# Spacing the rows of every output store 31 x 128 KiB apart instead of 31 x 4 KiB in a pairwise bilinear kernel

## The chip, the cores and the metric

The kernel runs on one core of one Trainium2 chip. The metric is the device time in microseconds (us). TensorE multiplies matrices, VectorE (DVE in profiles) works element by element, DMA engines move data; HBM is the memory off the cores, SBUF and PSUM are a core's own. Medians are quoted with the number of runs; runs are marked fast or slow, and only fast runs are compared.

## The reference

```python
# r_inputs: (4096, 32, 64) float32; W: (496, 64, 64) float32; 496 = pairs i < j of 32 fields
i_idx, j_idx = np.triu_indices(32, k=1)
vi = inputs[:, i_idx, :]
vj = inputs[:, j_idx, :]
vdotw = jnp.einsum('bpd,pde->bpe', vi, W)
y = (vdotw * vj).reshape(B, -1)          # (4096, 31744) float32
```

The output has 4096 rows of 31744 x 4 = 126,976 bytes, together 520.09 MB. The inputs that the kernel reads are 33.55 MB of x and 8.39 MB of weights. It is a kernel that mostly writes.

## The kernel before

A tile is 128 batch rows, one per partition; there are 32 tiles. Per tile TensorE transposes x and multiplies it with the weights into PSUM, DVE multiplies with the second field and writes the result into a ring in SBUF, and five stores (`STORES` groups the columns) take it from there. The parts that matter:

```python
STORES = [[0, 1], [2, 3], [4, 5], [6, 7, 8], [9, 10, 11, 12, 13, 14, 15]]
RING = 28160                    # float32 elements per partition, about 4.4 stores
# ... cut ...
    def load_x(t):
        xt = xbuf[t % 2]
        nc.scalar.dma_start(out=xt[:, : F * D], in_=x[ts(t, P), :])
        return xt
# ... cut: weights are loaded once, the first tile is transposed ...
    for t in range(NT):
        # ... cut: load of the next tile's x ...
        for s, group in enumerate(STORES):
            if at + store_w[s] > RING:
                at = 0
            osb = ring[:, at : at + store_w[s]]
            at += store_w[s]
            o0 = off[2 * group[0]]
            # ... cut: matmuls into PSUM, DVE products from PSUM and x into osb ...
            nc.sync.dma_start(out=out[ts(t, P), o0 : o0 + store_w[s]], in_=osb)
```

`out` is (4096, 31744), so partition p of tile t writes into batch row 128 t + p, and neighbouring partitions of a store write 124 KiB apart. This distance is called the pitch below.

## Time and profile before

| | before |
|---|---|
| median, 6 runs | 1339.76 us (1339.70 to 1339.98) |
| profiled span | 1338.1 us |
| DMA traffic | 562.89 MB, 421 GB/s over the span |
| share of the 16 DMA engines' time in packets | 92.7% stores and weights, 6.0% x loads |
| DVE busy | 1199.8 us, 90% |
| median landing of the largest store, 3776 KB | 21.9 us |

The lines are quoted and worked through in the prediction below.

### The profile page before, as it was taken

The page shows a single profiled execution, that of the slowest core. Times are in us where ns is not written, and L with a number is a line of the kernel's source. Part 1 is how long each engine was busy: PE and PEld are TensorE (multiplying, and loading weights), DVE is VectorE, ACT ScalarE, POOL GpSimd, SP SyncE. Part 2 cuts the span into 40 slices and gives each one's busy share as a digit, 9 for nine tenths or more (in the row PEclk, how much of TensorE's full clock was granted, in tenths as well). Part 3 has the DMA queues.
Part 4 walks back from the last instruction along what each step waited for, and adds up shares of the span by engine and source line. Part 5 has one row for each costly group of instructions (what it writes and reads, how often), then busy time and mean ns, then how long its engine had stood idle before and what let it go on. Part 6 is the DMA issues. An engine that isn't in the chain of part 4 may idle for free.

```text
span 1338.1 us, 13157 instructions
## 1 busy us (share of the span) xinstructions
PE 1142.4 (85%) x5376; PEld 511.0 (38%) x5376; DVE 1199.8 (90%) x1376; ACT 66.1 (5%) x65; POOL 0.9 (0%) x8
## 2 busy tenths in 40 slices
PE   7899788898988988988889888889788898988982
PEld 3344333343344433433333334434344333433431
DVE  6999899898899988999889989899898998998993
ACT  1000000000000000000000000000000000000000
POOL 0000000000000000000000000000000000000000
PEclk9999999999998999999999999999999999999996
DMA  9999999999999999999999999999999999999996
GB/s 393 427 430 433 431 427 435 424 428 432 430 430 428 424 425 430 421 429 430 416 427 415 428 433 403 429 422 423 430 418 411 431 417 432 411 424 432 422 424 272
DMA packets 30012, 562.89 MB, mean 421 GB/s; under 512 B 3456, under 2 KB 3840, under 8 KB 5376
## 3 DMA queue, kind: packets, MB, share of 16 engines
q1 hardware_dynamic: 25344, 528.49, 92.7%
q10 hardware_dynamic: 4608, 33.56, 6.0%
q8 instruction: 42, 0.69, 0.2%
q14 instruction: 18, 0.15, 0.0%
HBM read 41.94 MB, written 520.09 MB: 420 GB/s over the span
## 4 chain that ended last, share of the span: by engine, by line
DMA 41%; DVE 39%; PE 16%; issue 2%; DVEq 0%
DMA out_dram<-ring 41%; DVE ring L155 35%; PE pring L145 13%; DVE ring L164 4%; PE pring L102 3%; DMA x<-in_x_dram 1%; DVEq L155 0%; DVEq L164 0%
## 5 line engine op out<-in xcount | busy, mean ns | idle before, releaser
L155 DVE TENSOR_TENSOR ring<-pring,x 128x1024 f32<-128x1024 f32 (+3 forms) x1056 | 1115.8, 1102 | 115.3 <-DMA out_dram<-ring 55.9
L145 PE MATMUL pring<-w,xT 64*128 64x512 f32 (+4 forms) x4864 | 1077.5, 560 | 165.7 <-DVE ring L155 161.4
L145 PEld LDWEIGHTS pring<-w,xT 64*128 64x128 f32 x4864 | 452.5, 189 | 758.6 <-DVE ring L155 601.3
L103 ACT COPY xT<-pring 128x1024 f32<-128x1024 f32 x64 | 64.8, 1013 | 1193.8 <-PE pring L102 1193.8
L164 DVE TENSOR_TENSOR ring<-pring,x 128x64 f32<-128x64 f32 (+3 forms) x320 | 114.5, 383 | 3.7 <-DVE ring L155 0.5
L102 PE MATMUL pring<-ident,x 128*128 128x128 f32 x512 | 73.6, 290 | 8.5 <-DMA x<-in_x_dram 8.5
L102 PEld LDWEIGHTS pring<-ident,x 128*128 128x128 f32 x512 | 58.5, 147 | 46.9 <-issue 36.9
L103 ACT ACT_TABLE_LOAD x1 | 1.3, 1283 | 1.7 <-PEq L198 1.7
masks.py:199 POOL TENSOR_SCALAR_AFFINE_SELECT ident<-ident 128x128 f32<-128x128 f32 x1 | 0.3, 294 | 0.0
L78 POOL MEMSET x<- 128x64 f32 x2 | 0.2, 152 | 0.0
masks.py:197 POOL MEMSET ident<- 128x128 f32 x1 | 0.2, 205 | 0.3 <-POOLq L198 0.3
L198 POOL MEMSET const-bfloat16-1.0<- 128x1 bf16 x1 | 0.1, 102 | 0.0
L198 POOL MEMSET const-uint8-127<- 128x1 uint8 x1 | 0.1, 102 | 0.0
L198 POOL MEMSET const-float32-0.0<- 128x1 f32 x1 | 0.1, 99 | 0.2 <-issue 0.2
L198 POOL MEMSET const-float32-1.0<- 128x1 f32 x1 | 0.1, 99 | 0.0
## 6 DMA issues: line engine op xcount, KB each, us to landing
out_dram<-ring SPq DMA_DIRECT2D x32, 3776.0 KB, 21.9
out_dram<-ring SPq DMA_DIRECT2D x32, 3264.0 KB, 21.6
out_dram<-ring SPq DMA_DIRECT2D x32, 3168.0 KB, 22.4
out_dram<-ring SPq DMA_DIRECT2D x32, 2912.0 KB, 21.4
out_dram<-ring SPq DMA_DIRECT2D x32, 2752.0 KB, 22.0
x<-in_x_dram ACTq DMA_DIRECT2D x32, 1024.0 KB, 14.2
w<-in_w_dram SPq DMA_DIRECT2D x1, 992.0 KB, 7.5
w<-in_w_dram SPq DMA_DIRECT2D x1, 928.0 KB, 11.8
```

Source lines behind the costliest of these rows:

```text
L78: nc.gpsimd.memset(xb[:, F * D :], 0.0)
L102: nc.tensor.transpose(pt[:, ts(c, P)], xt[:, ts(n * g + c, P)], ident)
L103: nc.scalar.copy(xT[:, ts(g, 2 * BANK)], pt)
L145: nc.tensor.matmul(pm[:, h * half + b0 : h * half + b1], xT[h * D : (h + 1) * D, ts(p, P)], w_sb[p][h * D : (h + 1) * D, c0 + b0 : c0 + b1 ...
L155: nc.vector.tensor_tensor(runs(osb, o[0], o[1], n[0]), runs(pm, 0, half, n[0]), runs(xt, xj[0], xj[1], n[0]), ALU.mult,)
L164: nc.vector.tensor_tensor(osb[:, o[h] : o[h] + n[h]], pm[:, h * half : h * half + n[h]], xt[:, xj[h] : xj[h] + n[h]], ALU.mult,)
L198: nc = bacc.Bacc("TRN2", target_bir_lowering=False, num_devices=1)
```

## The change

Each partition takes 32 neighbouring batch rows, one per tile: partition p of tile t now owns batch row 32 p + t. The host reorders x so that each tile's load is still one contiguous 1 MB block, and the output is declared as (128, 32 x 31744), which is the same memory under another shape. The intent is to alter one thing only, the distance between the 128 rows of a store.

```diff
-    B = x.shape[0]
-    NT = B // P
+    NT = x.shape[0]
 ...
+    cols = sum(width)
 ...
-        nc.scalar.dma_start(out=xt[:, : F * D], in_=x[ts(t, P), :])
+        nc.scalar.dma_start(out=xt[:, : F * D], in_=x[t])
 ...
-            nc.sync.dma_start(out=out[ts(t, P), o0 : o0 + store_w[s]], in_=osb)
+            nc.sync.dma_start(out=out[:, t * cols + o0 : t * cols + o0 + store_w[s]], in_=osb)
 ...
-    x = np.ascontiguousarray(r_inputs).reshape(B, F * D)
+    NT = B // P
+    x = np.ascontiguousarray(r_inputs.reshape(P, NT, F * D).transpose(1, 0, 2))
 ...
-    o_d = nc.dram_tensor("out_0_dram", (B, NP * D), F32, kind="ExternalOutput").ap()
+    o_d = nc.dram_tensor("out_0_dram", (P, NT * NP * D), F32, kind="ExternalOutput").ap()
 ...
-    return r.results[0]["out_0_dram"]
+    return r.results[0]["out_0_dram"].reshape(B, NP * D)
```

## The prediction

> **What bounds the kernel now.** I read the page's head and its slices first, to see which resource never rests.
>
> ```profile
> span 1338.1 us, 13157 instructions
> PE 1142.4 (85%) x5376; PEld 511.0 (38%) x5376; DVE 1199.8 (90%) x1376; ACT 66.1 (5%) x65; POOL 0.9 (0%) x8
> ...
> DVE  6999899898899988999889989899898998998993
> ...
> DMA  9999999999999999999999999999999999999996
> GB/s 393 427 430 433 431 427 435 424 428 432 430 430 428 424 425 430 421 429 430 416 427 415 428 433 403 429 422 423 430 418 411 431 417 432 411 424 432 422 424 272
> DMA packets 30012, 562.89 MB, mean 421 GB/s; under 512 B 3456, under 2 KB 3840, under 8 KB 5376
> ```
>
> The DMA row stands at 9 in every slice but the last, and the GB/s row is flat near 427. DVE is busy too, but 10% of its time is free. So the candidate is DMA, and the table of queues says what fills it.
>
> ```profile
> q1 hardware_dynamic: 25344, 528.49, 92.7%
> q10 hardware_dynamic: 4608, 33.56, 6.0%
> q8 instruction: 42, 0.69, 0.2%
> ...
> HBM read 41.94 MB, written 520.09 MB: 420 GB/s over the span
> ```
>
> The shares add to 98.9% of 16 engines' span: 1323 us of 1338.1 are packets. Queue 1 is the stores and the weights, queue 10 the x loads. Queue 1's packets are 32 x 5 x 128 = 20480 store rows, 16 x 128 = 2048 weight rows, and 16 completions for each of 176 transfers, 2816: together 25344. So each row of a store is one packet, 520.09 MB / 20480 = 25.4 KB on average. Its speed: 528.49 MB / 16 = 33.03 MB per engine in 0.927 x 1338.1 = 1240 us is 26.6 GB/s per engine, 426 GB/s for sixteen. The x loads give 33.56 / 16 / (0.060 x 1338.1) = 26.1 GB/s, nearly the same, though they read rather than write. That both directions run at one speed speaks for the engines as the limit and against HBM.
>
> The waits agree that compute stands behind the stores.
>
> ```profile
> DVE ring L155 <- DMA out_dram<-ring: 55.9, 35, 3.0
> DVE ring L155 <- PE pring L145: 30.7, 27, 12.9
> ...
> PE pring L102 <- DMA x<-in_x_dram: 8.5, 1, 8.5
> ```
>
> DVE waits 35 times for a store to give back a piece of the ring; the only long wait for x is the first load. Last I asked for stretches, to find the 1.1% in which DMA rests (columns: PE, PEld, DVE, ACT, POOL busy, granted clock, DMA share, GB/s).
>
> ```profile
> 0.00:8.50 8.50, 0.00 (x0) 0.01 (x1) 0.00 (x0) 1.28 (x1) 0.88 (x8) 1.00 0.79 300
> 25.00:66.00 41.00, 36.80 (x180) 16.44 (x178) 39.83 (x47) 2.03 (x2) 0.00 (x0) 1.00 1.02 430
> 1319.00:1330.00 11.00, 0.00 (x0) 0.00 (x0) 0.00 (x0) 0.00 (x0) 0.00 (x0) 0.50 0.67 285
> 1330.00:1338.10 8.10, 0.00 (x0) 0.00 (x0) 0.00 (x0) 0.00 (x0) 0.00 (x0) 0.50 0.05 20
> ```
>
> Idle: 0.21 x 8.5 + 0.33 x 11 + 0.95 x 8.1 = 13 us, all at the first load and in the drain. In between DMA is full. So a microsecond added to every engine's store packets is a microsecond added to the time, and nothing saved on PE or DVE would show.
>
> **What the Trainium skill says.** Three places bear on this.
> 1. "DMA: Bandwidth & Descriptors", section Bandwidth ("Where 436 GB/s comes from"): sixteen ports of 32 bytes at 850 MHz give 435.2 GB/s, and its largest measured load, 16 MB, reached 425 GB/s. This trace agrees: 430 GB/s in the stretch from 25 to 66 us, and 426 inside queue 1's packets. The kernel is within about 2% of the ceiling (estimate: 426 against 435.2).
> 2. "HBM Reference", Specifications: about 716 GB/s for a pair of cores. The trace's 420 GB/s over the span is 59% of it, and only one core runs, so by this HBM has room. No run shows its own ceiling.
> 3. "DMA: Bandwidth & Descriptors", section "Latency and other measured facts", the row "HBM row pitch at large powers of two". It is the page that decides this case. Copies of [128 partitions x 16 KiB] from HBM to HBM, per direction: pitch 512 KiB 207 GB/s, 2 MiB 164, 4 MiB and 8 MiB 103, and 4 MiB plus 4 KiB 214, called full, while plus 192 bytes gave 97. It calls channel aliasing an inference. The trace before can't test it: its pitch is small.
>
> **The change part by part.**
> 1. *Instructions.* None is added or removed. The same matmuls, DVE products and 208 transfers, in the same order with the same waits: 0 us.
> 2. *x loads.* The host reorders x, so each tile is still one contiguous 1 MB with rows of 8 KB. Same bytes, same packets, 80 us of engine time as before: 0 us.
> 3. *Weights.* Untouched: 0 us.
> 4. *Stores.* Same 20480 rows, same lengths, still one packet each. Only the pitch moves. Before, 496 x 64 x 4 = 126,976 bytes = 31 x 4 KiB = 124 KiB. After, 32 times that: 4,063,232 bytes = 31 x 128 KiB = 3.875 MiB. A store's rows before lay in 15.5 MiB; after, they lie over 496 MiB.
> 5. *What the pitch costs.* The stores hold (520.09 / 528.49) x 1240 = 1221 us of each engine's time, all on the path. With s the share of full speed that they keep, the time grows by 1221 x (1/s - 1). For s I must read the skill's row. The 4 KiB pad healed a 4 MiB pitch, so neither distance nor the memory spanned is the trouble: it is what is left of the address once rows advance by a large power of two. The power of two inside the pitch is what counts in that reading. Ours is 31, an odd number, times 128 KiB, so it should behave like a pitch of 128 KiB, two steps of doubling below the 512 KiB that still gave 207 / 214 = 97%. I take 99.5 to 100%: 0 to 6 us, centre 2 us.
>
> Sum: 1339.8 + 0 + 0 + 0 + 2 = 1341.8, about 1342 us. I choose "nothing moves": "4 MB apart" sounds like the bad row of the skill's table, but it is 128 KiB short of 4 MiB, and the rest matters.
>
> **The rivals.**
> 1. *Half aliasing.* The skill's row is for copies, 214 read and 214 written. Here nearly all traffic is writes, 425 GB/s in one direction, and a write stream may lose sooner. If the loss at 512 KiB, 3%, holds here, it is 1221 x (1/0.97 - 1) = 38 us: 1378 us, 2.8% slower. For it: the engines have no slack to hide it. Against: the odd factor 31. A 6% loss gives 78 us, 1418 us.
> 2. *Full aliasing.* If size near 4 MiB counts and not its power of two, s = 103 / 214 = 0.48: 1221 x 1.08 = 1320 us more, 2660 us. At the 2 MiB row (0.77) it is 365 us more, 1705 us. Against: the 4 KiB pad restored everything at practically the same distance.
> 3. *Faster.* If today's 124 KiB pitch already costs HBM something, wider spacing could return it. At most the packets' 1323 us shrink to 562.89 MB / 435.2 = 1293 us, 30 us or 2.2%, and that would need every packet free of overhead. The slices' dips (403, 411) might be such losses; if half of the gap were, 1325 us. Against: loads and stores run at one speed, so it looks like the engines' own.
> 4. *Compute takes over.* Not possible through this change: DVE's 1199.8 us lie below, and DVE only waits more if stores slow down. It makes 0 us.
>
> **Range and chances.** The central reading gives 1339 to 1346, with three quarters of the weight. The slow side is long: partial aliasing of 3 to 5% has about 13%, worse than that about 10%. So the range is 1334 to 1400: it drops the heavy aliasing and keeps the mild. Faster by over 2% needs 1313 or less, which means hardly any overhead: 2%. Slower by over 2% means over 1366.6, an s under 0.978: 23%. Within 2%: 75%.
>
> **What would show each step.** If right: queue 1 keeps about 92.7% and queue 10 about 6.0% of the engines; the median store landing stays near 21.9 us for 3776 KB; GB/s stays near 427 in the middle slices; DVE's wait for stores stays near 56 us; PE and DVE busy times are unchanged. If aliasing: queue 1's share rises while its bytes are the same, the GB/s row falls evenly over all slices, store landings lengthen by the same factor, and DVE's wait for stores grows into its largest by the amount the span grows, as busy times stand still. If it were faster: the dips in the GB/s row go. What would make me wrong is the reading of the skill's row: that only the power of two within the pitch counts, which the trace before can't confirm. x loads are a control: their packets keep their time (about 80 us per engine) whatever the stores do, unless the stores hold HBM so busy that reads wait too.

## The result, and the profile after

The changed kernel took 1339.68 us (median of 6 runs, 1339.44 to 1339.88) against 1339.76 us. The ratio is 0.9999, 95% interval 0.9986 to 1.0012: the same.

From the page of the changed kernel: span, engines, the DMA and GB/s slices, the queues (packets, MB, share of 16 engines) and the largest store (KB, us to landing).

```profile
span 1337.9 us, 13157 instructions
PE 1146.6 (86%) x5376; PEld 516.0 (39%) x5376; DVE 1199.4 (90%) x1376; ACT 66.1 (5%) x65; POOL 0.9 (0%) x8
...
DMA  9999999999999999999999999999999999999996
GB/s 391 426 431 434 432 427 432 426 428 431 432 427 428 426 424 427 425 429 430 417 428 416 427 433 405 429 420 424 429 419 411 430 419 432 423 412 432 422 424 272
...
q1 hardware_dynamic: 25344, 528.49, 92.7%
q10 hardware_dynamic: 4608, 33.56, 6.0%
...
out_dram<-ring SPq DMA_DIRECT2D x32, 3776.0 KB, 21.9
```

And DVE's waits of the changed kernel (us in total, times, longest):

```profile
DVE ring L157 <- DMA out_dram<-ring: 51.2, 31, 3.0
DVE ring L157 <- PE pring L147: 35.6, 35, 13.1
```

The packets, their shares and the landing of the largest store are the same to the digit; DVE's wait for stores is 51.2 us against 55.9. Most dips of the GB/s row are in the same places in both kernels: 416 and 415 before, 417 and 416 after in slices 20 and 22, 403 and 405 in slice 25, 411 in slice 31 of both; one of 411 in slice 35 before stands in slice 36 after, as 412. Dips that repeat under quite different addresses are not put down to where in memory the rows lie; what makes them is not shown. Both kernels have 13157 instructions, the same number on every engine.

So the time is unmoved. What that leaves open is why: because the pitch is harmless for the reason given (the power of two inside it is only 128 KiB), or because a pitch never matters to a store at this rate, or because DMA is not the bound that it seems to be. The experiments separate these.

### The profile page after: what moved, and what is told of

It reads as the page before. It is cut to its first block, busy times and chain, and to the rows that moved or that the text cites. A ratio compares the mean times of both kernels' runs of the same rounds, so it can differ in the third digit from the quotient of the medians.

```text
span 1337.9 us, 13157 instructions
## 1 busy us (share of the span) xinstructions
PE 1146.6 (86%) x5376; PEld 516.0 (39%) x5376; DVE 1199.4 (90%) x1376; ACT 66.1 (5%) x65; POOL 0.9 (0%) x8
## 2 busy tenths in 40 slices
DMA packets 30012, 562.89 MB, mean 421 GB/s; under 512 B 3456, under 2 KB 3840, under 8 KB 5376
## 3 DMA queue, kind: packets, MB, share of 16 engines
q1 hardware_dynamic: 25344, 528.49, 92.7%
q10 hardware_dynamic: 4608, 33.56, 6.0%
## 4 chain that ended last, share of the span: by engine, by line
DMA 41%; DVE 38%; PE 17%; issue 2%; DVEq 0%
DMA out_dram<-ring 41%; DVE ring L157 35%; PE pring L147 14%; DVE ring L166 4%; PE pring L104 3%; DMA x<-in_x_dram 1%; DVEq L157 0%; DVEq L166 0%
## 5 line engine op out<-in xcount | busy, mean ns | idle before, releaser
L157 DVE TENSOR_TENSOR ring<-pring,x 128x1024 f32<-128x1024 f32 (+3 forms) x1056 | 1115.1, 1099 | 115.5 <-DMA out_dram<-ring 51.2
```

Of the source, the lines that this page charges most:

```text
L157: nc.vector.tensor_tensor(runs(osb, o[0], o[1], n[0]), runs(pm, 0, half, n[0]), runs(xt, xj[0], xj[1], n[0]), ALU.mult,)
```

## The experiments

Theory P, the prediction's: rows whose pitch holds a large power of two collide; 31 x 128 KiB behaves like 128 KiB, and 128 KiB is harmless. Rivals: N, a pitch costs stores nothing at all; D, distance or the span of memory counts; O, an odd factor is a cure of its own.

All pitch experiments share one edit to the changed kernel. The result tensor gets rows of 128 KiB instead of 124 (the last 4 KiB of each are never written, and the host slices them off), and a partition takes K neighbouring rows. K sets the pitch, a pad behind the K rows shifts it. Transfers, lengths and order stay the same, and every one of these results was correct.

```diff
+K = 32                       # 1, 4, 8, 16 or 32
+ROW = 32768                  # float32: 128 KiB
+PITCH = K * ROW + 0          # pad: 0, 256 (1 KiB), 1024 (4 KiB), 524288 (2 MiB)
 ...
-            nc.sync.dma_start(out=out[:, t * cols + o0 : t * cols + o0 + store_w[s]], in_=osb)
+            nc.sync.dma_start(out=out[t // K, :, (t % K) * ROW + o0 : (t % K) * ROW + o0 + store_w[s]], in_=osb)
 ...
-    x = np.ascontiguousarray(r_inputs.reshape(P, NT, F * D).transpose(1, 0, 2))
+    x = np.ascontiguousarray(r_inputs.reshape(NT // K, P, K, F * D).transpose(0, 2, 1, 3)).reshape(NT, P, F * D)
 ...
-    o_d = nc.dram_tensor("out_0_dram", (P, NT * NP * D), F32, kind="ExternalOutput").ap()
+    o_d = nc.dram_tensor("out_0_dram", (NT // K, P, PITCH), F32, kind="ExternalOutput").ap()
 ... cut: the host slices the pads off the result
```

### Is DMA the bound? x loaded only twice

```diff
-            xs[t + 1] = load_x(t + 1)
+            xs[t + 1] = load_x(t + 1) if t < 1 else xbuf[(t + 1) % 2]
```

> The changed kernel with x loaded for the first two tiles only and these two buffers used again by all later ones; wrong result on purpose, same stores, same compute. It tests whether the DMA engines bound the time. If they do, the 30 loads left out at 80.3/32 = 2.51 us of every engine each give back 75 us: 1264 us (1255 to 1285, as compute's 1199.8 us of DVE comes near). If the stores' path to memory alone or compute bounds it, 1340 us.

Measured: 1267.75 us (4 runs), ratio 0.9463; 72 us less. The result is wrong. From its page, the span, the slices and the queues, then one of its waits:

```profile
span 1266.1 us, 13067 instructions
...
DMA  9999999999999999999999999999999999999996
GB/s 392 426 431 433 430 431 432 429 429 429 416 424 426 426 420 423 424 423 423 423 427 419 418 430 422 421 424 414 422 425 427 420 416 420 419 422 430 420 418 283
...
q1 hardware_dynamic: 25344, 528.49, 97.8%
q10 hardware_dynamic: 288, 2.10, 0.4%
```

```profile
DVE ring L157 <- DMA out_dram<-ring: 2.0, 5, 1.2
```

The reads that were left out are given back nearly one for one (72 of 75 us), although the stores and the compute stayed as they were: queue 1 still takes 0.978 x 1266.1 = 1238 us of each engine, 1240 before. The time is the sum of what the DMA engines carry, reads and writes alike. A limit of the engines and one of a path to memory that reads and writes share would both look like this; no run tells them apart. Two more things show. The deepest dips of the GB/s row are gone, but dips of 414 and 416 remain, and the middle slices average 424 GB/s, no more than before (425): that the x loads cause the dips is not shown. And DVE hardly waits for a store any more (2.0 us against 51.2): here compute takes nearly as long as DMA.

### Pitch exactly 4 MiB

K = 32, no pad. It differs from the changed kernel's pitch by 128 KiB in 4 MiB.

> The changed kernel with every batch row of the result padded from 124 to 128 KiB, so that the 128 rows of a store lie exactly 4 MiB apart instead of 31 x 128 KiB; the pad is never written. Theory P (what counts is the largest power of two in the pitch): stores fall to about 103/214 = 0.48 of full speed, 1221 x 1.08 = 1320 us more, about 2660 us (2500 to 2900). Rival N (a pitch costs stores nothing at this rate; the Trainium skill's loss belongs to copies between HBM tensors): 1340 us, within 1%.

Measured: 2094.02 us (median of 4 runs, 2073.29 to 2105.89), ratio 1.566. The loss is 56 to 57%; 56.6% is used below. The profiled run is the fastest one. From its page:

```profile
span 2071.5 us, 13157 instructions
PE 1299.9 (63%) x5376; PEld 619.3 (30%) x5376; DVE 1210.9 (58%) x1376; ACT 66.1 (3%) x65; POOL 0.9 (0%) x8
...
DMA  9999999999999999999999999999999999999998
GB/s 313 202 212 233 211 243 270 284 276 268 276 270 274 296 280 265 277 276 290 293 257 274 276 295 283 287 259 274 300 279 271 280 266 298 286 274 286 294 296 225
...
q1 hardware_dynamic: 25344, 528.49, 93.8%
q10 hardware_dynamic: 4608, 33.56, 5.1%
...
out_dram<-ring SPq DMA_DIRECT2D x32, 3776.0 KB, 38.7
```

The DMA row is as full as before and moves a third less: same packets, same bytes, but queue 1 now takes 0.938 x 2071.5 = 1943 us of each engine instead of 1240, 703 us more. x loads, not touched, take 0.051 x 2071.5 = 106 us instead of 80, so their packets too take longer while such stores run. Together 729 of the 733 us by which the span grew. DVE's wait for stores is now its largest:

```profile
DVE ring L160 <- DMA out_dram<-ring: 736.2, 129, 15.7
```

It grew by 685 us over the changed kernel's, while DVE's own work grew by 11. A reader who saw only the DMA row of this page would call both kernels equally DMA-bound; the GB/s row beside it is what tells an engine that moves data from one that is held up. N falls: a store can lose a great deal to its pitch. P was right on the direction, and too high on the size: it said 2500 to 2900.

### Pitch 4 MiB + 4 KiB

K = 32, pad of 1024 elements.

> The same with 4 KiB more after each partition's 32 rows: a pitch of 4 MiB + 4 KiB. P: full speed again, 1340 us within 1%. A rival by which sheer distance or the span of memory counts (D): as slow as the 4 MiB pitch. N: 1340 us.

Measured: 1339.81 us (4 runs), ratio 1.0001. D falls: the rows lie as far apart as in the slow kernel, over as much memory, and nothing is lost.

### Pitch 512 KiB and pitch 128 KiB

K = 4 and K = 1, no pad.

> Padded rows of 128 KiB, but a partition takes 4 neighbouring batch rows instead of 32: pitch exactly 512 KiB. P, with the skill's 207/214: 3% on the stores, 38 us, about 1378 us (1345 to 1400). N: 1340 us.

> Padded rows of 128 KiB, one batch row per partition as in the kernel before: pitch exactly 128 KiB, the power of two that is left in the changed kernel's 31 x 128 KiB. P as the prediction used it: 1340 to 1346 us. If the odd factor 31 itself is what saved the changed kernel (rival O), a bare 128 KiB is slow: over 1366 us.

Measured: 1339.77 us, ratio 1.0000, and 1339.71 us, ratio 1.0000 (4 runs each). The bare 128 KiB is harmless without any odd factor, which is what step 5 of the prediction needs. The 38 us that P allowed for 512 KiB, and with it the premise of the prediction's first rival, are not there. These two kernels and the one with 4 KiB of pad also have the padded rows, so the padding itself costs nothing.

### Pitch 1 MiB and pitch 2 MiB

K = 8 and K = 16, no pad.

> Padded rows of 128 KiB, 8 neighbouring batch rows to a partition: pitch exactly 1 MiB, between 512 KiB (1.000 of the time before) and 2 MiB (1.0485). P with a loss that sets in gradually: 1.00 to 1.02, about 1345 us; a sharp threshold at 2 MiB: 1.000, 1340 us. Over 1.0485 would contradict the order by powers of two.

> Padded rows of 128 KiB, a partition takes 16 neighbouring batch rows: pitch exactly 2 MiB. The 4 MiB pitch cost 754 us against the skill's 1320, the 512 KiB pitch nothing, so the skill's sizes are too large here by about 0.57. P: 0.57 of the 365 us worked out from its 164/214, about 200 us: 1540 us (1400 to 1710). A rival by which only 4 MiB and more alias in a store (H): 1340 us.

Measured: 1350.94 us (4 runs), ratio 1.0080, interval 1.0064 to 1.0097: 0.8% slower, clear of noise. And 1405.24 us (median of three runs; a fourth, 1426.16 us, is slow), ratio 1.0485. The loss sets in gradually from 1 MiB, but steeply at the end: 0.8%, 4.8%, then 56.6% at 4 MiB. The 2 MiB figure lies within the range stated but far below its centre, 65 us rather than 200: one factor of 0.57 did not carry over from 4 MiB. From the page at 1 MiB:

```profile
span 1353.5 us, 13157 instructions
...
q1 hardware_dynamic: 25344, 528.49, 91.8%
q10 hardware_dynamic: 4608, 33.56, 6.6%
```

Queue 1 takes 0.918 x 1353.5 = 1242 us, only 2 more than before, and the x loads 89 us, 9 more. So at 1 MiB it is the reads beside the stores, and hardly the stores' own packets, that take longer; why is not shown.

### Pitch 6 MiB = 3 x 2 MiB

K = 32, pad of 524288 elements.

> The 4 MiB kernel with 2 MiB more after each partition's 32 rows: pitch 6 MiB = 3 x 2 MiB. P (the largest power of two inside the pitch decides, an odd factor changes nothing): the time of the 2 MiB pitch of the same call, within 5%. Rival D (distance, at least 4 MiB apart): as slow as 4 MiB or slower, 2090 us or more. Rival O (an odd factor undoes the aliasing whatever it multiplies): 1340 us. If 2 MiB itself costs nothing, P and O are not told apart.

Measured: 1402.60 us (4 runs), ratio 1.0484, against 1.0485 for 2 MiB. From its page:

```profile
span 1414.4 us, 13157 instructions
...
GB/s 379 385 389 409 414 403 398 396 417 413 402 410 391 402 427 392 408 401 385 401 403 399 396 386 396 413 395 402 390 397 411 390 394 401 393 404 415 399 419 293
...
q1 hardware_dynamic: 25344, 528.49, 92.2%
q10 hardware_dynamic: 4608, 33.56, 6.4%
```

The GB/s row is lower over the whole span, not in single dips. Queue 1 takes 0.922 x 1414.4 = 1304 us, 64 more than before, and the x loads 91 us, 10 more. This is the sharpest test of step 5: three times the distance of 2 MiB, half as far again as the 4 MiB that cost 56.6%, and the time is that of its power of two. D and O both fall; distance is not it, and the odd factor 3 neither helped nor hurt.

### Pitch 4 MiB + 1 KiB

K = 32, pad of 256 elements.

> The 4 MiB kernel with 1 KiB more per partition: pitch 4 MiB + 1 KiB. P taken to the letter (largest power of two in the pitch, here 1 KiB, as small as one likes) says 1340 us. The skill's row has 192 B not helping and 4 KiB healing; if a shift has to exceed some granule (G), 1 KiB lies in between and gives anything between 1340 and 2094 us, and P to the letter falls if it is over 1366.

Measured: 1437.36 us (4 runs), ratio 1.0729. So P to the letter is wrong: the largest power of two in this pitch is 1 KiB, and yet 7.3% are lost. How large the shift is matters: 1 KiB a row undoes most of the 56.6%, 4 KiB all of it. The reading that fits all these runs is that what counts is how far the rows are shifted against each other within the large power of two; "the power of two in the pitch" is then a short form that holds for pitches such as ours, whose rest is 128 KiB. No run shows in which part of the memory the rows meet.

### Why is 4 MiB cheaper than the skill's row? A shorter ring

After its first slice, the GB/s row of the 4 MiB kernel stands at 202 to 243 and then rises to 257 to 300. Theory L: streams collide when they advance in step, all engines in the same columns, and an engine that has fallen behind into an older store avoids the others (drift). Rival M: drift has nothing to do with it. A ring for two stores leaves little room for drift. The same edit on the changed kernel is the control.

```diff
-RING = 28160
+RING = 15104
```

> Control for the next run: the changed kernel with a ring of 15104 elements instead of 28160, so that only two stores can be under way or waiting at once and the 16 engines cannot run several stores apart. A store takes about 9 us of the engines and its compute about 8 us, so the queue may run dry now and then: 1340 to 1450 us.

> The 4 MiB kernel with the same small ring. In its profile stores ran at 202 to 243 GB/s in the first slices and at 270 to 300 later, when stores of different columns were under way at once. Theory L (the streams collide when they advance in step, and those that run apart collide less): with the small ring the rate stays at about 205 to 245 GB/s throughout, 562.89 MB / 0.225 = about 2500 us (2300 to 2750). Rival M (drifting apart has nothing to do with it, the first slices are slow for another reason): 2094 us plus what the control adds, so at most about 2200 us.

Measured: control 1647.02 us, ratio 1.2288; 4 MiB with the short ring 2853.38 us, ratio 2.1301 (4 runs each). Both are outside the ranges stated: the short ring itself costs 307 us, not up to 110, and at 4 MiB the time is over the 2750 that L allowed. From the page of the control, then of the short ring at 4 MiB:

```profile
DMA  9788878878787788778887888878888888787787
...
q1 hardware_dynamic: 25344, 528.49, 76.3%
```

```profile
span 2850.3 us, 13139 instructions
...
DMA  9889998989988899898898889988989899898898
GB/s 284 190 193 193 200 200 187 200 187 203 203 189 196 194 193 210 182 200 196 184 209 184 193 196 193 215 180 201 204 186 211 182 205 202 189 201 187 198 197 181
...
q1 hardware_dynamic: 25344, 528.49, 84.0%
```

In the control, queue 1's packets take 0.763 x 1641.7 = 1253 us, 1% more than with the long ring: what it lost is idle time between stores, not packet speed. At 4 MiB they take 0.840 x 2850.3 = 2394 us, 23% more than the 1943 us with the long ring, and the GB/s row never climbs. Rival M gives at most 2094 + 307 = 2401 us even with the control's real cost, 452 less than measured. So the depth of the queue of stores does matter once rows collide, as L says.

Whether the engines drift can be read from the packet records in the packed traces. The five stores of a tile have rows of five different lengths (22,016 to 30,208 bytes), so the size of a packet tells its store. Sampled every 0.5 us, at the moments with a store under way:

| kernel, stretch in us | store packets under way | of these, in one store | GB/s per engine in store packets |
|---|---|---|---|
| before, 50 to 200 | 14.9 | 14.0 | 26.9 |
| control, short ring, 50 to 1625 | 14.8 | 14.8 | 26.4 |
| 4 MiB, 50 to 200 | 15.4 | 14.4 | 12.8 |
| 4 MiB, 300 to 2050 | 15.0 | 8.2 | 17.5 |
| 4 MiB, short ring, 50 to 2830 | 14.8 | 14.6 | 13.7 |

(The third column counts the packets of the store that has most of them.) With nearly all engines in one store, 4 MiB rows go at 12.8 of 26.9, a share of 0.48, which is the share that theory P took for its 2660 us. Once the engines are spread over several stores, the rate is 17.5; the short ring keeps them together, and the rate low. Without the large pitch the same crowding costs next to nothing. So the drift is seen, and goes with the rate as L says. That it is the reason rests on this and on the short ring; no run holds the engines apart without changing something else.

## Why the prediction was right

**DMA as the bound.** Shown: leaving out 30 x loads gave back 72 of the 75 us that their packets took, and the losses at 2, 4 and 6 MiB were found as packet time, most of it of queue 1. Not shown is the prediction's finer reading, that the engines and not HBM are the limit: it rests on reads and writes running at one speed.

**Parts 1 to 3, nothing removed or added.** Shown by the page after: 25344 and 4608 packets, 92.7% and 6.0%, DVE 1199.4 us.

**Step 5, the pitch.** The step chose 0 to 6 us, centre 2, from the reading that 31 x 128 KiB behaves like 128 KiB. Measured -0.1 us; the 2 us allowance wasn't needed. The reading is supported on three sides: 128 KiB and 512 KiB without an odd factor cost nothing, 6 MiB costs what 2 MiB costs, and 4 MiB, reached by a mere 128 KiB more per partition, costs 56.6%. So the prediction was not right by luck: a pitch can matter a great deal to this kernel, and the reason given is what kept this one harmless. Where it was loose is its short form, as the 1 KiB pad showed, and its sizes: the 3% taken for 512 KiB measured nothing; for the 128 KiB rest of this change it makes no difference.

**Rival 1, half aliasing** (1378 us at 3%): its premise, a 3% loss at 512 KiB, is refuted here (1.0000). Its other worry, that a stream of writes alone loses sooner than copies do, was not borne out: with the long ring this kernel lost a smaller share at each pitch tried than the skill's row gives, and with the engines in one store about the same share at 4 MiB.

**Rival 2, full aliasing** (2660 us): it is real, but at exactly 4 MiB, and mis-sized. Its term 1221 x 1.08 = 1320 us measured 754. The share of 0.48 in it was right from 50 to 200 us, with the engines in one store; that they would spread out and speed up was not foreseen.

**Rival 3, faster** (1325 us or less): the dips of the GB/s row that it hoped to recover are nearly the same after the change, and at a pitch of 128 KiB too (416, 405 and 411 in slices 20, 25 and 31), so they do not come from the stores' pitch.

**The control in the prediction.** x loads were to keep their 80 us "unless the stores hold HBM so busy that reads wait too". In the changed kernel they keep it. At 4 MiB they took 106 us, so reads did take longer beside such stores; that it is HBM that they wait for is not shown.

No placement of the output that was tried beat the kernel before.

## What to carry to other kernels

This was seen with one core at work and stores from SBUF in rows of 21.5 to 29.5 KiB. When such a kernel lives on its stores, the pitch between the partitions' rows in memory looks free to choose as long as its rest against large powers of two is not small: 124 KiB, 128 KiB, 512 KiB, 31 x 128 KiB and 4 MiB + 4 KiB all ran at full speed here, 1 MiB lost 0.8%, 2 MiB and 6 MiB 5%, and exactly 4 MiB lost 57%. So take the pitch apart into an odd number and a power of two before judging it by its size, and if a layout lands on megabytes, try 4 KiB more per partition, which healed 4 MiB here. In the profile, read the GB/s row beside the DMA row: a full DMA row with fewer GB/s and the same packets is a store whose packets are held up, not a store with more to do.

## What the Trainium skill lacked or had wrong

- "DMA: Bandwidth & Descriptors", section "Latency and other measured facts", the row on row pitch: it measures copies between HBM tensors only and gives 207, 164 and 103 of 214 GB/s (3%, 23% and 52% less) at 512 KiB, 2 MiB and 4 MiB. For stores from SBUF, the whole kernel (562.89 MB, 92% of it stores) took 1.000, 1.0485 and 1.566 times as long, so the loss is smaller at each pitch. Only while nearly all engines were in one store did 4 MiB rows fall to the row's share: 12.8 of 26.9 GB/s per engine against 103 of 214. That +4 KiB heals it agrees: 1.0001.
- The same row says nothing of odd multiples, of 1 MiB, or of pads between 192 B and 4 KiB. Here 6 MiB cost what 2 MiB cost (1.0484 and 1.0485), 31 x 128 KiB cost nothing (0.9999), 1 MiB cost 0.8%, and a pad of 1 KiB on 4 MiB left 7.3%.
- No page says that the loss depends on how many stores are under way; the same row has lock-stepped streams only as an unverified inference. At 4 MiB, queue 1's packets took 1943 us per engine with room for about 4.4 stores and 2394 us with room for two, while without collisions the same edit moved them from 1240 to 1253 us.
